# Issuing the attention sums of two score units side by side in a two-layer decoder kernel

## The chip, the cores and the metric

The kernel runs on one core of a Trainium2 chip. A core has a matrix engine (TensorE, PE in the profile; its weight loads are listed as PEld), a vector engine (VectorE, DVE), a scalar engine (ScalarE, ACT), a general engine (GpSimd, POOL) and a queue processor that issues the transfers (SyncE, SP). Each takes its own instructions in order and waits for the others by semaphores. Matrix results land in PSUM, here used as eight banks of 128 partitions by 512 float32; everything else is in on-chip buffers, which the program takes from pools.

The metric is the device time of the whole program in microseconds, as the median of several runs. One further run was recorded by the profiler; its span reaches from the first to the last instruction.

## The reference

Two decoder layers work on `x` of shape (4, 1024, 256), with a context of 77 tokens for each batch:

```python
x = x + L0_attn(layernorm(x))            # 16 heads of 16, causal softmax with ALiBi, then w_proj
x = x + L0_xattn(layernorm(x), ctx)      # 16 heads of 64 over 77 context tokens
x = x + L0_ffn(layernorm(x))             # gated, ternary weights, int8-like activations
x = x + L1_attn(layernorm(x))            # 16 heads of 16, causal, "power" attention with gates
x = x + L1_xattn(layernorm(x), ctx)      # 8 heads of 64
x = x + L1_ffn(layernorm(x))             # gated, FP4 quantised
```

The change touches the two self-attentions. In layer 0 the weights of the values are `softmax(q k / 4 + bias)`. In layer 1 they are `(|q k| + 1e-7)^2 * G_t / G_s`, where G is a running product of gates, divided by their sum. In both, the output of a query is the sum of the values times these weights, over all earlier keys.

## The kernel before

**Stages.** The program goes through the batches twice. In the first phase it does layer 0's self-attention (`A0`) of batch b, interleaved with the cross-attention and the feed-forward of batch b-1 and with the preparation of weights. In the second phase it does layer 1's self-attention (`A1`), interleaved with the rest of layer 0 for the last batch and then with layer 1's cross-attention and feed-forward. Python generators yield after each small piece of work, and `weave` takes pieces of two generators in a given ratio. `schedule` lists who is woven with whom.

**What orders the instructions.** The interleaving only fixes the order in which instructions are written down. The program is then built by a tile framework with a scheduler that reorders each engine's instructions: it keeps what depends on data, on buffers and on explicit order edges, and among the rest picks by its own model of time. So the order on the engines is not that of the source.

**Score units.** A self-attention works on groups of four heads (g = 0 to 3) and on chunks of 256 queries (c = 0 to 3). For a chunk, each block of 128 keys (j) that it may see is one unit. The unit's scores, for keys by queries, are made for two heads at a time in a PSUM bank S (lines 392 to 394 in `A0`, 867 in `A1`). In `A0`, ScalarE takes the exponential into a buffer P (line 395). In `A1`, VectorE or ScalarE takes the absolute value into P (lines 873 and 871), ScalarE squares all of P (line 875), and for the two blocks at the diagonal POOL multiplies by a decay (line 878). P holds 4 heads by 256 queries and its pool has four buffers.

**Sums.** The function `pv` adds a unit to the result: for each of the four heads a matmul whose stationary operand is 32 columns wide, that head's values with a column of ones, and whose moving operand is P. Each head writes 32 of the 128 partitions of the PSUM bank O, so four matmuls stand beside each other in the array (line 404 in `A0`, line 895 in `A1`). The trace lists each of these float32 matmuls twice. In `A1`, off-diagonal sums use values that POOL has first scaled by gate factors: a memset and a multiplication into a buffer VsJ (lines 855 and 857), of which there are three. When the last unit of a chunk pair (`A0`) or a chunk (`A1`) has been added, `o_out` or `out` takes O out of PSUM, transposes and divides it.

**The lag.** A unit whose scores have been written down is put in the queue `pend`. Once there are more than two (`LAG0`, `LAG1`), the oldest is taken out and its `pv` is written down. This happens after each unit:

```python
for c, j in units:
    pend.append((pv, (c, j) + scores(c, j)))
    if len(pend) > self.LAG0:
        f, a = pend.popleft()
        f(*a)
    yield
```

In `A1` the same loop also calls `local`, which makes the exponentials of running gates for half of the queries (lines 831 and 832, read in `out`), as soon as the oldest waiting unit belongs to the new half.

Beside this, `A0` also computes the maxima of the next head group's scores (`a0_max`: matmuls at line 346, masks at 350, VectorE's maximum at 351), which go into the next group's exponent.

Of the kernel before, what the change touches and what calls it, by code (L numbers as in the profile page):

```python
# [89 lines left out]

class Kern:
    MAGIC = 12582912.0
    LAG0, LAG1 = 2, 2
    GQ, NQ = (2, 2, 2, 2), (12, 12, 12, 12)
    NW = ((25, 25, 38, 38),) * 4

# [26 lines left out]
        self.xs = {}  # L123
        self.ready = {}

    BUFS = {"X": 4, "V": 4, "QS": 2, "KS": 2, "P": 4, "ot": 2, "q4s": 2, "qr": 2, "VsJ": 3, "wst": 2, "E": 2, "kh": 1, "qp": 2, "EX": 2}


    BANKS = (
# [16 lines left out]
    def t(self, shape, dt, tag, alt=None):  # L146
        self.n += 1
        tag = (alt or {}).get(tag, tag)
        if tag[0] == "_":
            return self.sb.tile(shape, dt, tag=tag, name=f"s{tag}_{self.n}", bufs=2)  # L150
        return self.sb.tile(shape, dt, tag=tag, name=f"{tag}_{self.n}", bufs=self.BUFS.get(tag, 1))

# [226 lines left out]
    def a0_main(self, st, V, y, g, O, pend):  # L379
        nc = self.nc  # L380
        units = [(c, j) for c in range(4) for j in range(2 * c + 2)]

        def scores(c, j):
            q0 = max(j, 2 * c) * 128
            w = (2 * c + 2) * 128 - q0
            dg = j >= 2 * c
            P = self.t([128, 4, 256], F32, "P")
            for p in range(2):
                S = self.p("S").rearrange("p (h k) -> p h k", h=2)
                for e in range(2):  # L390
                    hh = 2 * p + e
                    nc.tensor.matmul(S[:, e, 0:w], st[1][:110, hh, j * 128 : (j + 1) * 128], st[0][:110, hh, q0 : q0 + w], start=e == 0, stop=not dg and e == 1)  # L392
                if dg:
                    nc.tensor.matmul(S[:, :, 0:128], self.identb, self.maskTb.unsqueeze(1).to_broadcast([128, 2, 128]), start=False, stop=True)
                nc.scalar.activation(P[:, 2 * p : 2 * p + 2, 256 - w :], S[:, :, 0:w], AF.Exp)  # L395
            return P, 256 - w

        def pv(c, j, P, o0):
            if c % 2 == 0 and j == 0:
                O[0] = self.p("O")  # L400
            o = (c % 2) * 256
            for hh in range(4):
                h = g * 4 + hh
                nc.tensor.matmul(O[0][hh * 32 : hh * 32 + 32, o + o0 : o + 256], V[j // 4][:, j % 4, h * 17 : h * 17 + 32], P[:, hh, o0:], start=c % 2 == 0 and j == 0, stop=c % 2 == 1 and j == 2 * c + 1)  # L404
            if c % 2 == 1 and j == 2 * c + 1:
                self.o_out(O[0], y, g, c // 2)

        for c, j in units:
            pend.append((pv, (c, j) + scores(c, j)))
            if len(pend) > self.LAG0:  # L410
                f, a = pend.popleft()
                f(*a)
            yield

    def o_out(self, O, y, g, ch):
# [400 lines left out]
    def a1_main(self, b, V, dr, gt, cs):  # L816

        nc = self.nc
        ew, W, DL, DR, ub = gt
        Ds, O, st = {}, {}, {}  # L820
        chunks = [(g, c) for g in range(4) for c in cs]

        def load_gates(g, c, new):
            if new:
                for s in range(2):
                    nc.sync.dma_start(DL[s][3:15], W[g].rearrange("p (h j) n -> (p h) (j n)", h=4))
            nc.sync.dma_start(DR[0:3].rearrange("k h j t -> k h (j t)"), W[g].rearrange("p (h j) n -> p h (j n)", h=4)[:, :, c * 256 : c * 256 + 256])

        def local(g, k):
            S = self.p("D")  # L830
            nc.tensor.matmul(S, self.ind, DL[0][:, k * 512 : (k + 1) * 512], start=True, stop=True)
            nc.scalar.activation(ub, S, AF.Exp)

        def decay(g, c):
            Dt = self.t([128, 2, 4, 128], F32, "y1")
            for k in range(2):
                j = 2 * c + k
                pd = self.p("D").rearrange("p (h t) -> p h t", h=4)
                for s in range(2):
                    q = slice(s * 64, s * 64 + 64)  # L840
                    nc.tensor.matmul(pd[:, :, q], DL[s][:, j * 128 : (j + 1) * 128], DR[:, :, k, q], start=s == 0, stop=s == 1)
                nc.scalar.activation(Dt[:, k], pd, AF.Exp)
            Ds[g, c] = Dt

        def scores(g, c, j):
            hs = slice(g * 4, g * 4 + 4)
            q0 = max(j, 2 * c) * 128
            w = (2 * c + 2) * 128 - q0
            P = self.t([128, 4, 256], F32, "P")
            i0 = max(j + 1, 2 * c)  # L850
            ni = 2 * c + 2 - i0
            Vs = None
            if ni:
                Vs = self.t([128, 2, 83], F32, "VsJ")
                nc.gpsimd.memset(Vs[:, :ni, 68:83], 0.0)
                o = self.eo(j) + i0 - j - 1
                nc.gpsimd.tensor_tensor(
                    Vs[:, :ni, 0:68].rearrange("p i (h e) -> p i h e", h=4),
                    V[j // 4][:, j % 4, g * 68 : g * 68 + 68].rearrange("p (h e) -> p h e", h=4).unsqueeze(1).to_broadcast([128, ni, 4, 17]),
                    ew[:, o : o + ni, hs].unsqueeze(3).to_broadcast([128, ni, 4, 17]),  # L860
                    ALU.mult,
                )
            for p in range(2):
                S = self.p("S").rearrange("p (h k) -> p h k", h=2)
                for e in range(2):
                    hh = 2 * p + e
                    nc.tensor.matmul(S[:, e, 0:w], st[g][1][:96, hh, j * 128 : (j + 1) * 128], st[g][0][:96, hh, q0 : q0 + w], start=e == 0, stop=e == 1)  # L867
                Pv = P[:, 2 * p : 2 * p + 2, 256 - w :]
                self.absn += 1
                if self.absn % 8 in ABS_ACT:  # L870
                    nc.scalar.activation(Pv, S[:, :, 0:w], AF.Abs)
                else:
                    nc.vector.tensor_reduce(Pv, S[:, :, 0:w].unsqueeze(3), AX.X, ALU.max, apply_absolute_value=True)  # L873
            Pw = P[:, :, 256 - w :]
            nc.scalar.activation(Pw, Pw, AF.Square, bias=self.eps1)  # L875
            if j >= 2 * c:
                Pd = P[:, :, 256 - w : 384 - w]
                nc.gpsimd.tensor_tensor(Pd, Pd, Ds[g, c][:, j - 2 * c], ALU.mult)  # L878
            return P, Vs, i0

        def pv(g, c, j, P, Vs, i0):
            if j == 2 * c:
                O[g, c] = self.p("O")
            Oc = O[g, c]
            fin = (c > 0 and j == 2 * c - 1) or (c == 0 and j == 1)
            for i in range(max(j, 2 * c), 2 * c + 2):
                c0 = (i - 2 * c) * 128
                for hh in range(4):
                    h = g * 4 + hh
                    r = slice(hh * 32, hh * 32 + 32)  # L890
                    if i == j:
                        lhs, o0 = V[j // 4][:, j % 4, h * 17 : h * 17 + 32], 256 + c0
                    else:
                        lhs, o0 = Vs[:, i - i0, hh * 17 : hh * 17 + 32], c0
                    nc.tensor.matmul(Oc[r, o0 : o0 + 128], lhs, P[:, hh, c0 : c0 + 128], start=j == 2 * c and i == 2 * c, stop=fin and i == 2 * c + 1)  # L895
            if fin:
                out(g, c)
# [20 lines left out]
        pend = deque()  # L918
        need = None
# [3 lines left out]
        for n, (g, c) in enumerate(chunks):  # L923
            units = [2 * c, 2 * c + 1] + list(range(2 * c))
            nxt = chunks[n + 1] if n + 1 < len(chunks) else None
            if nxt and nxt[0] == g:
                load_gates(*nxt, False)
            if c == cs[0] and g < 3:
                st[g + 1] = self.stacks(g + 1, dr, False)
            if c % 2 == 0:  # L930
                need = (g, c // 2)
            for m, j in enumerate(units):
                pend.append((g, c, j) + scores(g, c, j))
                if len(pend) > self.LAG1:
                    pv(*pend.popleft())
                if need and (pend[0][0], pend[0][1] // 2) == need:
                    local(*need)
                    need = None
                if nxt:
                    if nxt[0] != g and m == 1:  # L940
                        load_gates(*nxt, True)
                    if m == (len(units) - 1 if nxt[0] != g else min(3, len(units) - 1)):
                        decay(*nxt)
                yield
        while pend:
            pv(*pend.popleft())
            yield

# [320 lines left out]
```

## Time and profile before

| | us |
|---|---|
| median of 3 runs | 2577.97 (2571.63 to 2580.77) |
| profiled execution | 2593.41 |
| its span | 2591.4 |
| TensorE busy | 2214.7 (85% of the span) |
| VectorE busy | 1769.4 (68%) |
| ScalarE busy | 1592.7 (61%) |
| POOL busy | 1227.5 (47%) |
| stage of `A0`'s sums, 164 to 1355 us | TensorE busy 1070.28 of 1191 |
| stage of `A1`'s sums, 1355 to 2445 us | TensorE busy 917.87 of 1090 |

Busy time counts an engine's instructions where they overlap only once. "Idle before" is the time that an engine stood still just ahead of an instruction, with what ended it; "issue" there means that the profile shows nothing that was waited for. The chain of waits is followed back from the last instruction to whatever released each one, so that its parts add up to the span. A line such as L189 can be that of a helper: L189 is the three-term matmul of split float32 operands that projections, cross-attention and feed-forward all use.

### The profile page before, as it was taken

How to read it: one execution, taken by the hardware profiler on the slowest of the kernel's cores; microseconds unless marked ns; L12 is line 12 of the kernel's file. 1: busy time of each engine (PE TensorE's matmuls, PEld its weight loads, DVE VectorE, ACT ScalarE, POOL GpSimd, SP SyncE). 2: the span in 40 equal slices, each digit the busy share in tenths (PEclk: the TensorE clock that was granted, in tenths of full speed). 3: DMA queues.
4: the chain of work that ended last, by engine and by line, in shares of the span. 5: the costliest groups of instructions: out<-in, count | busy, mean ns of one | idle time of the engine just before them, and what ended most of it. 6: DMA issues, size and time to landing. Idle time of an engine off the chain costs nothing.

```text
span 2591.4 us, 51361 instructions
## 1 busy us (share of the span) xinstructions
PE 2214.7 (85%) x19057; PEld 1575.9 (61%) x19094; DVE 1769.4 (68%) x3865; ACT 1592.7 (61%) x4099; POOL 1227.5 (47%) x2026
## 2 busy tenths in 40 slices
PE   5698889988989999899887997798879887879887
PEld 4455446754556755566545774476667666757676
DVE  3556555667566577566777677678857886677787
ACT  3255435666656676556666996786658674867532
POOL 6121302144321242213446467657875677565665
PEclk9689889999999999999997998898989998979888
DMA  8856540223652225122262211521162215333000
GB/s 228 184 133 178 163 103 13 68 62 108 158 146 58 67 81 183 41 68 55 73 189 80 73 53 64 168 83 47 64 167 72 57 65 165 86 111 83 10 9 17
DMA packets 170287, 248.44 MB, mean 96 GB/s; under 512 B 13734, under 2 KB 146166, under 8 KB 161430
## 3 DMA queue, kind: packets, MB, share of 16 engines
q1 hardware_dynamic: 170038, 245.17, 34.9%
q8 instruction: 150, 2.46, 0.4%
q14 instruction: 99, 0.81, 0.1%
HBM read 162.65 MB, written 82.21 MB: 94 GB/s over the span
## 4 chain that ended last, share of the span: by engine, by line
PE 50%; DVE 17%; DMA 13%; POOL 7%; ACT 5%; issue 3%; SPq 1%; POOLq 0%; ACTq 0%; DVEq 0%
PE T L189 8%; PE W L189 7%; PE O L404 6%; PE Q L189 4%; PE M L346 4%; PE S L392 4%; PE O L895 4%; PE S L867 3%; DMA KS<-c_alk 2%; DVE P L873 2%; DMA MD<-R 2%; DVE s_mt L351 2%; DMA UD<-R 1%; DMA QS<-dr 1%; PE T L716 1%
## 5 line engine op out<-in xcount | busy, mean ns | idle before, releaser
L351 DVE TENSOR_REDUCE s_mt<-M 128x1 f32<-128x512 f32 (+3 forms) x608 | 386.4, 656 | 161.7 <-PE M L350 112.8
L395 ACT ACTIVATE P<-S 128x512 f32<-128x512 f32 (+1 forms) x640 | 342.0, 564 | 167.5 <-PE S L392 87.1
L875 ACT ACTIVATE P<-P,eps 128x1024 f32<-128x1024 f32 (+1 forms) x320 | 341.6, 1091 | 68.5 <-DVE P L873 66.0
L873 DVE TENSOR_REDUCE P<-S 128x512 f32<-128x512 f32 (+1 forms) x480 | 281.4, 609 | 62.9 <-PE S L867 55.5
L189 PE MATMUL T<-R,xX 128*128 128x308 f32 (+1 forms) x1328 | 303.6, 340 | 13.2 <-DMA R<-g1d 3.1
L346 PE MATMUL M<-KS,QS 108*128 108x512 bf16 (+3 forms) x768 | 229.5, 347 | 54.7 <-DVE s_mt L351 21.3
L616 POOL TENSOR_TENSOR E<-E,s_xsm 128x616 f32<-128x616 f32 x88 | 108.3, 1231 | 323.5 <-DVE s_xsm L614 209.3
L392 PE MATMUL S<-QS,KS 110*128 110x256 bf16 (+1 forms) x1280 | 232.0, 270 | 27.9 <-ACT P L395 14.3
L613 ACT ACTIVATE E<-T,s_xmx 128x77 f32<-128x77 f32 x704 | 223.9, 361 | 41.4 <-DVE s_xmx L610 35.5
L189 PEld LDWEIGHTS T<-R,xX 128*128 128x128 f32 x1328 | 221.3, 197 | 42.4 <-ACT E L613 8.7
L189 PE MATMUL W<-R,xph 128*128 128x256 f32 (+2 forms) x1192 | 241.2, 299 | 4.3 <-DVE xpl L178 3.3
L867 PE MATMUL S<-QS,KS 96*128 96x256 bf16 (+1 forms) x1280 | 213.3, 273 | 35.1 <-DVE P L873 24.8
L404 PE MATMUL O<-P,V 128*32 128x256 f32 (+1 forms) x2560 | 241.4, 376 | 0.0
L189 PEld LDWEIGHTS W<-R,xph 128*128 128x128 f32 (+2 forms) x1192 | 195.0, 200 | 17.0 <-DVE xpl L178 4.9
L878 POOL TENSOR_TENSOR P<-P,y 128x512 f32<-128x512 f32 x128 | 168.2, 1320 | 68.0 <-ACT P L875 40.5
L189 PE MATMUL W<-R,xpl 128*128 128x256 f32 (+2 forms) x596 | 178.4, 299 | 3.3 <-DVE xpl L178 3.2
L392 PEld LDWEIGHTS <-KS 110*128 110x128 bf16 x1280 | 105.2, 100 | 110.2 <-issue 54.2
L867 PEld LDWEIGHTS <-KS 96*128 96x128 bf16 x1280 | 104.1, 100 | 102.3 <-issue 73.4
L613 ACT ACTIVATION_READ_ACCUMULATOR E<-T,s_xmx 128x1 f32 x704 | 166.1, 242 | 0.0
L177 ACT ACTIVATE xph<-W 104x128 fp32r<-104x128 f32 (+1 forms) x228 | 102.4, 475 | 97.1 <-PE W L627 35.3
L895 PE MATMUL O<-P,VsJ 128*32 128x128 f32 x3584 | 157.0, 282 | 5.3 <-ACT P L875 3.5
L346 PEld LDWEIGHTS <-QS 108*128 108x128 bf16 x768 | 69.4, 102 | 131.7 <-issue 103.2
(357 smaller groups left out, 5493.3 us busy)
## 6 DMA issues: line engine op xcount, KB each, us to landing
QS<-dr SPq DMA_DIRECT2D x72, 384.0 KB
KS<-dr SPq DMA_DIRECT2D x72, 384.0 KB
dr<-qp SPq DMA_DIRECT2D x32, 768.0 KB
MD<-R SPq DMA_DIRECT2D x24, 616.0 KB
UD<-R SPq DMA_DIRECT2D x24, 616.0 KB
R<-MD SPq DMA_DIRECT2D x22, 616.0 KB
R<-UD SPq DMA_DIRECT2D x22, 512.0 KB
R<-g1d SPq DMA_DIRECT2D x6, 1408.0 KB
```

The lines of the kernel that those rows point to most:

```text
L189: nc.tensor.matmul(out, x, y, start=first and n == 0, stop=last and n == len(seq) - 1)
L346: nc.tensor.matmul(Sv[:, x, 0:w], QS[:108, hh, i * 128 : (i + 1) * 128], KS[:108, hh, k0:k1], start=x == 0, stop=not diag and x == n - 1)
L351: nc.vector.tensor_reduce(out, Sv[:, :, 0:w], AX.X, ALU.max)
L392: nc.tensor.matmul(S[:, e, 0:w], st[1][:110, hh, j * 128 : (j + 1) * 128], st[0][:110, hh, q0 : q0 + w], start=e == 0, stop=not dg and e == 1)
L395: nc.scalar.activation(P[:, 2 * p : 2 * p + 2, 256 - w :], S[:, :, 0:w], AF.Exp)
L404: nc.tensor.matmul(O[0][hh * 32 : hh * 32 + 32, o + o0 : o + 256], V[j // 4][:, j % 4, h * 17 : h * 17 + 32], P[:, hh, o0:], start=c % 2 = ...
L613: nc.scalar.activation(E[:, n * 77 : (n + 1) * 77], Sv[:, k, :], AF.Exp, bias=mx[:, n : n + 1], accum_out=sm[:, n : n + 1])
L867: nc.tensor.matmul(S[:, e, 0:w], st[g][1][:96, hh, j * 128 : (j + 1) * 128], st[g][0][:96, hh, q0 : q0 + w], start=e == 0, stop=e == 1)
L873: nc.vector.tensor_reduce(Pv, S[:, :, 0:w].unsqueeze(3), AX.X, ALU.max, apply_absolute_value=True)
L875: nc.scalar.activation(Pw, Pw, AF.Square, bias=self.eps1)
L878: nc.gpsimd.tensor_tensor(Pd, Pd, Ds[g, c][:, j - 2 * c], ALU.mult)
L895: nc.tensor.matmul(Oc[r, o0 : o0 + 128], lhs, P[:, hh, c0 : c0 + 128], start=j == 2 * c and i == 2 * c, stop=fin and i == 2 * c + 1)
```

## The change

There are three edits.

- After a unit's scores, nothing is taken from `pend` until four units wait in it (`LAG + PAIR`). Then the two oldest are summed, one after the other. So pairs are written down at every second unit.
- The two sums are traced inside `issue_after`, with the newest unit's last score matmul (`self.lead`). It adds order edges for the scheduler: what the block puts on TensorE must stand behind that matmul in TensorE's order. The edge concerns issue order alone; there is no semaphore, and other engines are not touched. In `A1`, `local` is now called inside the block, just ahead of the first sum that belongs to the new half, and also when the queue is emptied at the end.
- The pool VsJ has five buffers instead of three, since up to four units wait with their scaled values.

```diff
-    LAG0, LAG1 = 2, 2
+    LAG0, LAG1, PAIR = 2, 2, 2
...
-    BUFS = {"X": 4, ..., "P": 4, ..., "VsJ": 3, ...}
+    BUFS = {"X": 4, ..., "P": 4, ..., "VsJ": 5, ...}
...
-                    nc.tensor.matmul(S[:, e, 0:w], st[1][:110, hh, ...
+                    self.lead = nc.tensor.matmul(S[:, e, 0:w], st[1][:110, hh, ...
                 if dg:
-                    nc.tensor.matmul(S[:, :, 0:128], self.identb, ...
+                    self.lead = nc.tensor.matmul(S[:, :, 0:128], self.identb, ...
...
-            if len(pend) > self.LAG0:
-                f, a = pend.popleft()
-                f(*a)
+            if len(pend) >= self.LAG0 + self.PAIR:
+                with self.tc.issue_after(self.lead.ins):
+                    for _ in range(self.PAIR):
+                        f, a = pend.popleft()
+                        f(*a)
...
-                    nc.tensor.matmul(S[:, e, 0:w], st[g][1][:96, hh, ...
+                    self.lead = nc.tensor.matmul(S[:, e, 0:w], st[g][1][:96, hh, ...
...
-                if len(pend) > self.LAG1:
-                    pv(*pend.popleft())
-                if need and (pend[0][0], pend[0][1] // 2) == need:
-                    local(*need)
-                    need = None
+                if len(pend) >= self.LAG1 + self.PAIR:
+                    with self.tc.issue_after(self.lead.ins):
+                        for _ in range(self.PAIR):
+                            if need and (pend[0][0], pend[0][1] // 2) == need:
+                                local(*need)
+                                need = None
+                            pv(*pend.popleft())
...
         while pend:
+            if need and (pend[0][0], pend[0][1] // 2) == need:
+                local(*need)
+                need = None
             pv(*pend.popleft())
```

More of the change, by code (lines that the diff above doesn't have):

```diff
@@ L124, in __init__ @@
         self.ready = {}
-    BUFS = {"X": 4, "V": 4, "QS": 2, "KS": 2, "P": 4, "ot": 2, "q4s": 2, "qr": 2, "VsJ": 3, "wst": 2, "E": 2, "kh": 1, "qp": 2, "EX": 2}
+    BUFS = {"X": 4, "V": 4, "QS": 2, "KS": 2, "P": 4, "ot": 2, "q4s": 2, "qr": 2, "VsJ": 5, "wst": 2, "E": 2, "kh": 1, "qp": 2, "EX": 2}
     BANKS = (
@@ L391, in scores @@
                     hh = 2 * p + e
-                    nc.tensor.matmul(S[:, e, 0:w], st[1][:110, hh, j * 128 : (j + 1) * 128], st[0][:110, hh, q0 : q0 + w], start=e == 0, stop=not dg and e == 1)
+                    self.lead = nc.tensor.matmul(S[:, e, 0:w], st[1][:110, hh, j * 128 : (j + 1) * 128], st[0][:110, hh, q0 : q0 + w], start=e == 0, stop=not dg and e == 1)
                 if dg:
-                    nc.tensor.matmul(S[:, :, 0:128], self.identb, self.maskTb.unsqueeze(1).to_broadcast([128, 2, 128]), start=False, stop=True)
+                    self.lead = nc.tensor.matmul(S[:, :, 0:128], self.identb, self.maskTb.unsqueeze(1).to_broadcast([128, 2, 128]), start=False, stop=True)
                 nc.scalar.activation(P[:, 2 * p : 2 * p + 2, 256 - w :], S[:, :, 0:w], AF.Exp)
@@ L866, in scores @@
                     hh = 2 * p + e
-                    nc.tensor.matmul(S[:, e, 0:w], st[g][1][:96, hh, j * 128 : (j + 1) * 128], st[g][0][:96, hh, q0 : q0 + w], start=e == 0, stop=e == 1)
+                    self.lead = nc.tensor.matmul(S[:, e, 0:w], st[g][1][:96, hh, j * 128 : (j + 1) * 128], st[g][0][:96, hh, q0 : q0 + w], start=e == 0, stop=e == 1)
                 Pv = P[:, 2 * p : 2 * p + 2, 256 - w :]
```

## The prediction

> **What bounds the kernel now.** I read the page first, then the chain of waits by stage, then the busy time by stage, and last the time line of TensorE around the instructions that the change moves. From the page:
>
> ```profile
> span 2591.4 us, 51361 instructions
> PE 2214.7 (85%) x19057; PEld 1575.9 (61%) x19094; DVE 1769.4 (68%) x3865; ACT 1592.7 (61%) x4099; POOL 1227.5 (47%) x2026
> L404 PE MATMUL O<-P,V 128*32 128x256 f32 (+1 forms) x2560 | 241.4, 376 | 0.0
> L895 PE MATMUL O<-P,VsJ 128*32 128x128 f32 x3584 | 157.0, 282 | 5.3 <-ACT P L875 3.5
> ```
>
> TensorE (PE) is the busiest engine. The sums that the change moves are L404 (layer 0, called A0 here) and L895 (layer 1, A1; 1024 more of its matmuls stand under O<-P,V with 59.1 us). The two stages, cut where L404 ends at 1355 us (busy time by stretch, and the chain of waits for each of the same stretches, shares of the stretch):
>
> ```profile
> core 0: us, PE busy (x) PEld busy (x) DVE busy (x) ACT busy (x) POOL busy (x), PEclk, DMA share, GB/s
> 164.00:1355.00 1191.00, 1070.28 (x8347) 687.86 (x8370) 773.97 (x1681) 711.20 (x2017) 346.72 (x493) 0.94 0.38 101
> 1355.00:2445.00 1090.00, 917.87 (x9473) 704.64 (x9480) 796.95 (x1787) 780.30 (x1818) 726.54 (x1327) 0.91 0.31 87
> ```
>
> ```profile
> by line: PE O L404 12.1%; PE S L392 8.1%; PE M L346 8.0%; PE Q L189 7.1%; PE T L189 6.6%; PE W L189 6.4%; DMA KS<-c_alk 5.3%; DMA MD<-R 4.5%; DVE s_mt L351 3.6%; DMA UD<-R 2.8%; issue 2.4%; PE T L716 2.3%; PE M L350 1.9%; PE S L394 1.7%; PE
> ```
>
> The reader is to see two things. In A0 TensorE is busy 1070 of 1191 us while VectorE and ScalarE have a third free; and the first entry of the chain there is L404 itself, 12.1% of 1191 = 144 us. In A1 (84% busy) the same chain gives L895 8.7% of 1090 = 95 us, with VectorE, POOL and transfers taking larger parts.
>
> Why L404 is dear is in the time line of TensorE (start, length, instruction, count). The first seven lines are from A0, the last four from A1:
>
> ```profile
> 999.85 0.38 PE L392 MATMUL S<-QS,KS 110*128 110x256 bf16 x2
> 1000.16 0.41 PE L404 MATMUL O<-P,V 128*32 128x128 f32 x2
> 1000.50 0.38 PE L189 MATMUL Q<-WAh,yTh 128*128 128x256 f32 x1
> ...
> 1010.11 0.28 PE L392 MATMUL S<-QS,KS 110*128 110x128 bf16 x2
> 1010.23 0.27 PE L394 MATMUL S<-maskTb,identb 128*128 128x256 bf16 x1
> 1010.43 0.64 PE L404 MATMUL O<-P,V 128*32 128x256 f32 x8
> 1011.00 0.39 PE L392 MATMUL S<-QS,KS 110*128 110x256 bf16 x2
> ...
> 2006.53 0.27 PE L909 MATMUL U<-ident,ot 128*128 128x128 f32 x1
> 2006.73 0.43 PE L895 MATMUL O<-P,V 128*32 128x128 f32 x8
> 2006.97 0.40 PE L895 MATMUL O<-P,VsJ 128*32 128x128 f32 x8
> 2007.31 0.39 PE L867 MATMUL S<-QS,KS 96*128 96x256 bf16 x2
> ```
>
> These are narrow matmuls (128*32: 32 columns of the array, four beside each other). Each stands twice in the trace, since 1280 in the program give 2560 rows. Ordinary matmuls follow each other every 0.11 us here, but between the last ordinary one and the first narrow one pass 0.20 us (1010.23 to 1010.43), and on the way back at least 0.20 us more. One whole unit, 8 rows of 256 columns, takes 1010.23 to 1011.00 = 0.77 us.
>
> **The change, part by part.** *What is added and removed.* No arithmetic: the built programs have the same 15,499 matmuls, and equal counts on every other engine and on SP. Only order and two buffers differ, so the price is one of order.
>
> *Fixed cost of a run.* Call narrow matmuls that follow each other a run. Over the runs of the trace, the median from the last ordinary start to the next ordinary start is 0.559 us for 8 rows of 128 columns (37 runs), 0.786 for 16 (115, as at 2006.53 to 2007.31), and 0.997 for 24 (28). Each further set of 8 rows so costs 0.215 us, which leaves 0.344 us fixed; 8 rows of 256 columns (0.774, 194 runs) agree: 0.344 + 0.430. An ordinary matmul would take 0.11 us of the 0.344, so one run less saves 0.235 us.
>
> *Number of runs.* I compared the order of TensorE's instructions in both built programs. A0: 401 runs before, 191 after. Before, 124 runs have only 2 of a unit's 4 matmuls and 24 have only one; 238 have 4. After, 135 runs have 8, two whole units. A1: 262 before, 235 after, because most runs there were whole units already and are mixed.
> - Fixed: 210 x 0.235 = 49.4 us in A0, 27 x 0.235 = 6.3 us in A1.
> - Streaming: two of four tiles take as long as four (2 matmuls of 256 columns: 0.754 us, 16 runs). With the widest tile of each run at 0.215 us per 128 columns, A0's runs stream 154.6 us before and 132.9 after, A1's 129.9 and 128.4: 21.7 + 1.5 us.
> - Sum of TensorE time: 71.1 us in A0, 7.8 us in A1.
>
> [...] (waits: who, for what, us in all, times, longest):
>
> ```profile
> PEld O L404 <- issue: 78.3, 382, 0.4
> PEld O L895 <- issue: 33.0, 153, 0.7
> ```
>
> 382 times the narrow weight load of L404 waited 0.2 us for nothing else that the profile shows. I take the row's 0.235 us. [...]
>
> *What of it lies on the path.* L404 is 144 us of the chain and 232.4 us of busy time in its stage, 62%. L895 is 95 of 192.6 us, half. So 71.1 x 0.62 + 7.8 x 0.5 = 44 + 4 = 48 us. The rest lies beside what the chain shows as transfers (KS<-c_alk alone 5.3% of A0) or VectorE, and none of those gets shorter.
>
> *The added wait.* Sums now stand behind the newest unit's last score matmul. In the built order of A0 a unit's sums stood behind the scores of one later unit (299 of 320), afterwards behind two or three (156 each). Queued behind the waiting matmul on TensorE is everything else: side work and the next scores. That matmul waits for its score bank, which the exponential at L395 empties; TensorE waited 14.3 us for that in all. I cost this at nothing because the wait existed before; what is new is that no sums can fill it, at most those 14.3 us again.
>
> *The P buffers.* P has four buffers. Three were held at most (two pending and the newest), now four, so the exponential of the next unit needs the P that the oldest pending sum frees. In A0 the wait of ACT for L404 at L395 does not appear among the waits at all; in A1 it is 16.1 us already (ACT P L871 12.7, DVE P L873 3.4, both for L895). Lower bound 0, upper bound treated as the slower rival; I take 0 in A0, since sums stand on TensorE ahead of the scores that need the buffer, and a few us in A1.
>
> *Five VsJ buffers.* POOL's memset L855 waits 160.9 us (102 times) for L895 with three buffers. A longer lag with three could not work; with five the wait should shrink. On the chain the two lines of VsJ have 9.6 us. Bounds: 0 to 10 us gained; I take 3, which cancels the few us of P.
>
> *local(), moved ahead of the first sum of its pair.* Up to 16 times (first chunk of each head group and batch) its exponential, 0.63 us at L832, and its matmul, 0.3 us, can stand right before a use: 0 to 15 us, taken as 0, since VectorE has other work. The O bank changes no owner within a pair: 6, 14 and the A1 chunks' 2c+2 units are all even.
>
> Sum: 2591.4 - 48 = 2543 us of span, 2545 with the 2 us around it (profiled run 2593.4). The median shown is 2578.0, 0.6% below that run; so 2578 - 48 = 2530.
>
> **The rivals.**
> 1. *All of it arrives* (78.9 us, and VsJ's 10): 2490. For: A0's TensorE is 90% busy. Against: 225 us of A0's chain are transfers.
> 2. *Others take the bound*: with TensorE faster, the maxima at L351 (386 us of VectorE, 161.7 us idle before) and the exponentials hold the pace, or the whole new order, which the scheduler drew up afresh on all engines, eats it. About 10 us remain: 2568.
> 3. *Slower: P runs out.* P is written, squared (L875, 1.09 us), for diagonals multiplied on POOL (L878, 1.32 us), and only then summed. With no buffer in reserve, A1's writers L873 and L871 wait for the sums, and the sums for the newest scores. It cancels the gain from 48/320 = 0.15 us per A1 unit on; today it is 16.1/320 = 0.05. At five times today's, 80 us, minus 48 plus the 16 there: 2594; I put 2600. Against: the average unit in A1 was already summed 2 to 3 units later, and the built order moves that little (47 to 58 matmuls in between).
> 4. *The change does little*, because the scheduler had paired already: true of A1, excluded for A0 by the run counts.
>
> **How the numbers follow.** Half of it arrives: 0.50, 2530, own range 2508 to 2556. All: 0.17, around 2490. Absorbed: 0.14, 2556 to 2586. Slower: 0.19, around 2600 with a tail to 2650. A measurement here tells 0.3% (8 us) from no change. Faster: 0.50 + 0.17 + half of 0.14 = 0.74; same: 0.07; slower: 0.19. The range 2485 to 2605 leaves out some 0.07 below and 0.09 above.
>
> **What would show it.** Right: L404's busy time near 241 - 35 us, PEld O L404 <- issue at about half of its 382 times, A0's stretch shorter by some 45 us and A1's by under 10; POOL's wait at L855 well under 160.9. Wrong: A0 as long as before with PE idle more (rival 2); ACT P L395 or DVE P L873 waiting for PE O (rival 3); or the transfers KS<-c_alk and MD<-R growing on the chain.

## The result, and the profile after

The changed kernel takes 2591.4 us (median of 8 runs, 2588.4 to 2605.9) against 2577.7 us (8 runs, 2571.6 to 2584.0): the ratio is 1.0062, interval 1.0044 to 1.0081. It is slower by 0.6%, where 2530 us had been forecast.

The page after the change:

```profile
span 2588.7 us, 51317 instructions
PE 2148.5 (83%) x19094; PEld 1596.3 (62%) x19094; DVE 1752.9 (68%) x3865; ACT 1595.8 (62%) x4099; POOL 1223.3 (47%) x2026
L404 PE MATMUL O<-P,V 128*32 128x256 f32 (+1 forms) x2560 | 178.3, 374 | 2.7 <-ACT P L395 2.7
L897 PE MATMUL O<-P,VsJ 128*32 128x128 f32 x3584 | 154.0, 284 | 4.6 <-ACT P L877 4.6
```

TensorE is busy 66 us less than in the trace shown before (2214.7), and 51 us less than in a second trace of the kernel before (2199.1, below). L404 is 63 us less than in either. From the waits, the narrow loads of layer 0 and POOL's wait for the sums (lines behind layer 0's loop stand two further down in this kernel: L895 and L855 are L897 and L857):

```profile
PEld O L404 <- issue: 41.4, 198, 0.5
POOL VsJ L857 <- PE O L897: 159.4, 113, 6.1
```

382 waits of the narrow load have become 198. The time line of TensorE shows a pair: sixteen rows of 256 columns in one run, with 1.20 us from the last full matmul's start (1010.21) to the next one's (1011.41):

```profile
1010.21 0.27 PE L394 MATMUL S<-maskTb,identb 128*128 128x256 bf16 x1
1010.41 1.07 PE L404 MATMUL O<-P,V 128*32 128x256 f32 x16
1011.41 0.39 PE L346 MATMUL M<-KS,QS 108*128 108x512 bf16 x1
```

Two runs of one unit took 2 x 0.77 us. So the saving on TensorE is real, and yet the program is longer. The first profiled execution of the kernel before was itself 21 us longer than the second, so the stages are compared with the second. Busy time by stage, of the kernel before (second execution), cut where layer 0's last sum leaves PSUM, where layer 1's last does, and at the end:

```profile
153.00:1336.00 1183.00, 1066.30 (x8402) 682.56 (x8427) 779.45 (x1693) 715.56 (x2027) 348.27 (x495) 0.95 0.37 103
1336.00:2425.00 1089.00, 916.34 (x9461) 706.28 (x9472) 795.69 (x1785) 779.55 (x1817) 725.01 (x1326) 0.91 0.31 87
2425.00:2571.00 146.00, 109.98 (x675) 102.08 (x674) 117.80 (x229) 44.67 (x146) 91.64 (x104) 0.87 0.03 12
```

and after the change:

```profile
151.00:1329.00 1178.00, 1022.31 (x8426) 711.13 (x8425) 773.87 (x1696) 712.01 (x2025) 348.58 (x496) 0.93 0.38 103
1329.00:2433.00 1104.00, 916.05 (x9466) 708.40 (x9466) 788.56 (x1786) 785.01 (x1816) 724.72 (x1325) 0.91 0.31 86
2433.00:2589.00 156.00, 112.58 (x676) 105.99 (x676) 114.44 (x223) 45.49 (x146) 88.00 (x104) 0.82 0.03 11
```

The columns are the stretch, its length, then busy time of PE, PEld, DVE, ACT and POOL, the granted clock, the share of the DMA engines and GB/s. There are two questions. In layer 0's stage TensorE is busy 44 us less, but the stage is only 5 us shorter. In layer 1's stage it is busy as long as before, and the stage is 15 us longer; the end takes 10 more, so that 25 us are lost behind layer 0.

### The profile page after: what moved, and what is told of

It is laid out like the page before. It is cut to its first block, busy times and chain, and to the rows that moved or that the text cites. A ratio compares the mean times of both kernels' runs of the same rounds, so it can differ in the third digit from the quotient of the medians.

```text
span 2588.7 us, 51317 instructions
## 1 busy us (share of the span) xinstructions
PE 2148.5 (83%) x19094; PEld 1596.3 (62%) x19094; DVE 1752.9 (68%) x3865; ACT 1595.8 (62%) x4099; POOL 1223.3 (47%) x2026
## 4 chain that ended last, share of the span: by engine, by line
PE 46%; DVE 19%; DMA 18%; POOL 7%; ACT 6%; issue 3%; SPq 1%; POOLq 0%; ACTq 0%; DVEq 0%
PE T L189 8%; PE W L189 8%; PE O L404 5%; PE Q L189 4%; PE S L392 3%; PE O L897 3%; DMA MD<-R 3%; PE M L346 3%; PE S L869 3%; DMA UD<-R 3%; DMA KS<-c_alk 2%; DVE P L875 2%; DVE s_mt L351 2%; DMA y<-locd 2%; DMA QS<-VsJ 1%
## 5 line engine op out<-in xcount | busy, mean ns | idle before, releaser
L395 ACT ACTIVATE P<-S 128x512 f32<-128x512 f32 (+1 forms) x640 | 338.6, 567 | 118.3 <-PE S L394 64.8
L392 PE MATMUL S<-QS,KS 110*128 110x256 bf16 (+1 forms) x1280 | 232.4, 269 | 45.4 <-DMA QS<-VsJ 23.6
L189 PE MATMUL W<-R,xph 128*128 128x256 f32 (+2 forms) x1192 | 249.1, 306 | 10.0 <-DVE xpl L178 8.3
L189 PEld LDWEIGHTS W<-R,xph 128*128 128x128 f32 (+2 forms) x1192 | 202.5, 207 | 18.7 <-DVE xpl L178 9.7
L392 PEld LDWEIGHTS <-KS 110*128 110x128 bf16 x1280 | 111.4, 101 | 119.2 <-issue 48.5
L189 PE MATMUL W<-R,xpl 128*128 128x256 f32 (+2 forms) x596 | 183.6, 308 | 1.4 <-DVE xpl L178 1.4
L404 PE MATMUL O<-P,V 128*32 128x256 f32 (+1 forms) x2560 | 178.3, 374 | 2.7 <-ACT P L395 2.7
L615 ACT ACTIVATION_READ_ACCUMULATOR E<-T,s_xmx 128x1 f32 x704 | 160.8, 230 | 0.0
L177 ACT ACTIVATE xph<-W 128x512 fp32r<-128x512 f32 (+1 forms) x228 | 99.9, 469 | 97.9 <-PE W L629 34.8
L897 PE MATMUL O<-P,VsJ 128*32 128x128 f32 x3584 | 154.0, 284 | 4.6 <-ACT P L877 4.6
```

What stands on the lines that cost most here:

```text
L189: nc.tensor.matmul(out, x, y, start=first and n == 0, stop=last and n == len(seq) - 1)
L392: self.lead = nc.tensor.matmul(S[:, e, 0:w], st[1][:110, hh, j * 128 : (j + 1) * 128], st[0][:110, hh, q0 : q0 + w], start=e == 0, stop=no ...
L615: nc.scalar.activation(E[:, n * 77 : (n + 1) * 77], Sv[:, k, :], AF.Exp, bias=mx[:, n : n + 1], accum_out=sm[:, n : n + 1])
```

## The experiments

Each ratio below is to runs of the kernel before that were measured together with that experiment; their medians lie between 2573.6 and 2584.0 us. So ratios can be compared between experiments, and microseconds only within one.

### A second trace of the kernel before

> The kernel before, profiled a second time. Its first profiled execution took 2593.4 us, 15 us over its median of 2578, while the changed kernel's profiled execution (2590.6) is at its median of 2591. If the first trace was a slow one, this one has a span near 2576 and its stages (layer 0's attention ends at 1356 us in the first trace) end earlier; then part of the 26 us by which layer 0's attention seemed shorter after the change is not the change's. If it is again near 2590, the stage times of the first trace stand.

It took 2572.5 us with a span of 2570.3. Layer 0's last sum left PSUM at 1336.2 us instead of 1356.2. So of the 27 us that the first trace shows between the two kernels at that point, 20 belong to that one execution.

### Which part of the change is slower

The two loops are independent in the built order: with one of them changed, the other layer's runs on TensorE are those of the kernel before or nearly so. Layer 0 alone (this edit and the next are against the changed kernel):

```diff
             if len(pend) >= self.LAG0 + self.PAIR:      # layer 0: as changed
...
-                if len(pend) >= self.LAG1 + self.PAIR:
...
+                if len(pend) > self.LAG1:               # layer 1: as before
+                    pv(*pend.popleft())
...
-    BUFS = {..., "VsJ": 5, ...}
+    BUFS = {..., "VsJ": 3, ...}
```

> Pairs and order edges in layer 0's attention only; layer 1's loop and the three VsJ buffers as before. Built order: A0 191 narrow runs, A1 264. Theory 1 (A0 gains, A1's pairing and what follows it give the gain back): about 26 us faster than before, ratio near 0.990. Theory 2 (A0's gain is spent wherever it is made, since the second phase is held by other engines and by the order drawn up afresh): within 8 us of before, ratio 0.997 to 1.003. Theory 3 (A0's pairing is itself the loss, and the first trace only hid it): slower, ratio 1.005 or more.

Measured: 2566.9 us, ratio 0.9983 (0.9965 to 1.0000). It is not slower, and it gains 4 us by the ratio (8 by the medians) rather than 26. The number is theory 2's; its reason, that the second phase spends the gain, is not borne out: the gain is already missing at the end of layer 0's own stage (below).

Layer 1 alone, with five VsJ buffers:

```diff
-            if len(pend) >= self.LAG0 + self.PAIR:
...
+            if len(pend) > self.LAG0:                   # layer 0: as before
+                f, a = pend.popleft()
+                f(*a)
```

> Pairs and order edges in layer 1's attention and five VsJ buffers; layer 0's loop as before. Built order: A0 401 narrow runs as before, A1 237. Theory 1: slower by 15 to 40 us, ratio 1.006 to 1.015, because the held-back sums keep P buffers, and VectorE's and ScalarE's waits at the lines that write P grow. Theory 2: within 8 us of before. Theory 3: equal or slightly faster, ratio 0.995 to 1.000.

Measured: 2611.8 us, ratio 1.0152 (1.0130 to 1.0175), 37 to 39 us slower. The loss is made in layer 1. That P buffers are its cause, as the expectation said, is not borne out below. The two halves do not add up: minus 4 and plus 39 us would make 35, and the whole change loses 16. Why the loss is smaller in company is open.

The buffers alone:

```diff
-    BUFS = {..., "VsJ": 3, ...}
+    BUFS = {..., "VsJ": 5, ...}
```

> The kernel before with five VsJ buffers and nothing else. Built order: A0 401 narrow runs, A1 278. Theory 1: within 5 us of before; POOL's wait at its memset for the sums, 160.9 us with three buffers, stays above 100 us, as it did in the changed kernel with five (159.4), so that the loss is the pairing's. Rival: the two more buffers alone change layer 1's order for the worse, 10 us or more slower.

Measured: 2570.3 us, ratio 0.9985 (0.9970 to 0.9999), and POOL's wait at the memset was 175.0 us in layer 1's stage, more than with three (158.8 in the second trace). The buffers are not the loss. Nor do they shorten the wait they seemed made for: over the whole program it is 159 to 184 us in the kernels with three buffers and 149 to 182 in those with five. What sets it is open.

### What in layer 1 is slower

The changed kernel without its order edges:

```diff
-                with self.tc.issue_after(self.lead.ins):
+                if True:
...
-                    with self.tc.issue_after(self.lead.ins):
+                    if True:
```

> The changed kernel without its order edges: pairs are written down, five VsJ buffers, but the scheduler may put a sum wherever it likes. Built order: A0 401 narrow runs as before, A1 271. Theory P (in layer 1 the edge holds sums behind scores, so that buffers and outputs come late, and this costs the 37 us): the loss goes with the edge, within 8 us of before. Rival L (the loss is in local() now standing right ahead of its first use, or in the source order of pairs): still slower by 20 us or more, since local() and the pairs are written down as in the changed kernel.

Measured: 2576.0 us, ratio 1.0008 (0.9992 to 1.0024). The loss is gone. So is the effect in layer 0: the built order has 401 runs there again, as many as before. Writing two sums down together does nothing by itself; only the edge makes a pair.

Then the place of `local`. Layer 1's pairs with their edges and layer 0 as before, but `local` outside the edge and before the pair is due:

```diff
                     with self.tc.issue_after(self.lead.ins):
                         for _ in range(self.PAIR):
-                            if need and (pend[0][0], pend[0][1] // 2) == need:
-                                local(*need)
-                                need = None
                             pv(*pend.popleft())
+                if need and (pend[0][0], pend[0][1] // 2) == need:
+                    local(*need)
+                    need = None
...                                                     # nor when the queue is emptied
```

> Layer 1's pairs with their edges and five VsJ buffers, layer 0 as before, but local() is called outside the edge, after a pair has been taken out, when the oldest waiting unit belongs to the new half, as in the kernel before. With the late local() this took 2611.8 us, ratio 1.0152. Rival L: most of the 37 us comes back, ratio under 1.005, ScalarE's wait for local's matmul (ACT y L832 <- PE D L831, 17.7 us) is gone. Theory P: the loss stays, ratio 1.010 or more.

Measured: 2578.6 us, ratio 1.0022 (1.0011 to 1.0034). Of the 1.52%, 1.30% (33 us) came back from moving one matmul and one exponential, which the program does 32 times. The stage of layer 1 is 1122 us with the late `local` and 1083 with the early one, at nearly the same TensorE work (923 and 919 us). The waits of ScalarE and VectorE that bear on it, first with the late `local`, then with the early one, and last ScalarE's wait for `local` in the changed kernel (L834 there):

```profile
ACT y L832 <- PE D L831: 17.7, 13, 6.1
ACT P L871 <- PE O L895: 17.1, 14, 3.8
DVE P L873 <- PE O L895: 10.6, 15, 2.7
```

```profile
ACT P L871 <- PE O L895: 43.4, 17, 8.5
DVE P L873 <- PE O L895: 4.7, 8, 1.8
ACT y L832 <- PE D L831: 2.0, 4, 0.7
```

```profile
ACT y L834 <- PE D L833: 12.9, 9, 4.3
```

Line 832 is `local`'s exponential and 831 its matmul. Behind the edge the matmul stands on TensorE after the newest unit's scores; the exponential, already at the head of ScalarE's queue, waits for it up to 6.1 us (up to 4.3 in the changed kernel), and ScalarE starts nothing of what stands behind it: the traces of the kernel before and of the changed one have ScalarE's work in the order of the built program (2047 and 2042 entries, alike neighbours counted once, none out of place). The kernel before had 2.0 us of this wait in all. Worked out from the traces, the result of `local` lay ready a median of 9.6 us before its first reader in the kernel before, 10.7 us with the early `local`, and 4.9 us with the late one. The lines at 871 and 873 are the waits for a free P: they are longer where the kernel is faster (48.1 us against 27.7). P was not what cost.

Two things limit this account. The 17.7 us are about half of the 33, and 12.9 of the changed kernel's 19; the rest was not found in any one wait. And a late result alone does not cost: in the changed kernel without edges it lay ready a median of 7.5 us before its reader (4.5 with the edges), for the first chunk of a head group only 1.2 us (1.0), and that kernel is at 1.0008.

Is it the edge, or that `local` is written down later? The same kernel with `local` at the late place, but outside the edge:

```diff
                 if len(pend) >= self.LAG1 + self.PAIR:
+                    if need and (pend[0][0], pend[0][1] // 2) == need:
+                        local(*need)
+                        need = None
                     with self.tc.issue_after(self.lead.ins):
                         for _ in range(self.PAIR):
-                            if need and (pend[0][0], pend[0][1] // 2) == need:
-                                local(*need)
-                                need = None
                             pv(*pend.popleft())
```

> Layer 1's pairs with their edges and five VsJ buffers, layer 0 as before. local() is written down at the late place, just ahead of its pair, but outside the edge, so that the scheduler may issue its matmul earlier than the newest scores. If the edge on local()'s matmul is the loss: near the early local(), ratio under 1.006. If the late place in the source is enough: near 1.015, as with the edge.

Measured: 1.0046 (1.0034 to 1.0057), so 1.06% of the 1.30% is the edge on `local`'s matmul; the 0.24% left for the later place is little more than the intervals can tell from nothing.

And the other way round, the kernel before with `local` alone made late and held, no pairs and three buffers:

```diff
                 if len(pend) > self.LAG1:
+                    if need and (pend[0][0], pend[0][1] // 2) == need:
+                        with self.tc.issue_after(self.lead.ins):
+                            local(*need)
+                        need = None
                     pv(*pend.popleft())
-                if need and (pend[0][0], pend[0][1] // 2) == need:
-                    local(*need)
-                    need = None
...                                                     # and when the queue is emptied
```

> The kernel before with nothing but local() moved: traced just ahead of the first sum of the new half and held by the edge behind the newest unit's scores. No pairs, three VsJ buffers. If the late local() costs its 33 us by itself, ratio 1.008 or more and ScalarE waits at L832 for local's matmul well over 2.0 us. If it takes the pairs to make it late enough to hurt, within 8 us of before.

Measured: 1.0065 (1.0039 to 1.0091), 17 us, which lies between the two forecasts. It costs by itself, though half of what it costs among layer 1's pairs. ScalarE's own wait at L832 was only 4.2 us here, against the forecast of "well over 2.0", so most of the 17 us is not that wait. In seven of the 32 cases the reader takes the result within 0.04 us of its end; the trace shows 1.6 us of waiting for it there. What the rest consists of is open.

Last, the whole change with `local` put back (the edit of the early `local`, in the changed kernel):

> The changed kernel with one thing put back: local() is called outside the edge, after a pair has been taken out, as before. The changed kernel is 1.0062 of before. If the place of local() inside the edge is the whole of the loss, layer 0's pairs (0.9983) and layer 1's pairs with the early local() (1.0022) add up to about 1.000: 2568 to 2582 us, at least 10 us faster than the changed kernel. If it was the two kinds of pairs together, it stays above 1.004.

Measured: 0.9990 (0.9974 to 1.0006). The place of `local`, in the edge or out of it, is the whole of the loss: 0.72%, 19 us. What is left is a change that saves TensorE 42 us in its trace (2157.4 against 2199.1) and the program nothing that can be measured.

### Where layer 0's saving went

TensorE in layer 0's stage, before and with layer 0's pairs alone. Before, in the second trace, it was busy 1066.30 of 1183 us (the row 153.00:1336.00 above). What it waited for there:

```profile
PE M L346 <- DVE s_mt L351: 19.7, 32, 3.5
PE M L346 <- DMA KS<-c_alk: 19.1, 6, 5.6
PE S L392 <- ACT P L395: 12.3, 17, 3.6
PE S L392 <- DMA QS<-VsJ: 11.9, 4, 4.1
```

With layer 0's pairs, busy time by stretch and waits:

```profile
152.00:1328.00 1176.00, 1017.15 (x8399) 709.01 (x8422) 773.17 (x1695) 710.78 (x2024) 348.01 (x494) 0.93 0.38 103
```

```profile
PE M L346 <- DMA KS<-c_alk: 33.9, 7, 6.2
PE S L392 <- DMA QS<-VsJ: 22.5, 5, 5.8
PE M L346 <- DVE s_mt L351: 22.0, 44, 3.2
PE S L392 <- ACT P L395: 21.8, 24, 3.9
```

Busy time fell by 49 us and the stage by 7; the other 42 are idle. One pair of traces is thin evidence for 7 us, since two traces of the kernel before differ by more than that. Worked out from all kept traces with the loads in place, from the first to the last time that layer 0's sums leave PSUM: the eight without pairs in layer 0 take 1183 to 1199 us, the four with pairs 1177 to 1182. On average the stage is 11 us shorter, TensorE is busy 50 us less and idle 39 us more.

The transfers KS<-c_alk, the last of a head group's load of queries and keys, and QS<-VsJ, the two rows of maxima, hold TensorE 25 us longer, in about as many waits as before (12 against 10), and the exponentials 10 us longer. One such load, before and then with layer 0's pairs, in the time lines of the transfer queue and of TensorE:

```profile
1099.97 0.78 SPq L317 DMA_DIRECT2D QS<-dr  x2
1112.06 0.38 PE L346 MATMUL M<-KS,QS 108*128 108x128 bf16 x4 [1.77 <-DMA KS<-c_alk]
```

```profile
1095.97 0.77 SPq L317 DMA_DIRECT2D QS<-dr  x2
1108.11 0.58 PE L346 MATMUL M<-KS,QS 108*128 108x128 bf16 x4 [4.71 <-DMA KS<-c_alk]
```

The load is issued as TensorE's matmuls on the buffers' former content end (in the first trace of the kernel before ten such loads, and in the changed kernel's eight, start within 0.1 us of the end of the L394 that they wait for), and its first reader starts 12.1 us later in both. What differs is how much of the 12.1 us TensorE fills with other work. Over all waits for KS<-c_alk in the stage the median from issue to reader is 12.1 us before (6 cases) and 12.2 with pairs (7). If the narrow runs had only been covering loads of a fixed duration, the saving must appear once there are none. Two kernels leave the loads out for 14 of layer 0's 16 head groups, which then compute with other heads' values:

```diff
     def stacks(self, g, dr, alibi):
+        if alibi:
+            self.held = getattr(self, "held", [])
+            self.turn_s = getattr(self, "turn_s", -1) + 1
+            if len(self.held) == 2:
+                return self.held[self.turn_s % 2]
...
             nc.sync.dma_start(KS[96:110], self.c["alk"][:, g * 4 : g * 4 + 4, :])
+            self.held.append((QS, KS))
```

> The kernel before, leaving out the loads of the stacked queries and keys for 14 of layer 0's 16 head groups (the first two groups' are used again), so that these groups compute with other heads' values. No transfer is left to wait for at the start of a group except the two rows of maxima. Together with the next kernel it asks where layer 0's gain went. Expected 25 to 60 us faster than before (KS<-c_alk has 62 us of the chain in layer 0's stage); this alone tells no theory from another.

> Layer 0's pairs alone, with the same loads left out as in the kernel above. With the loads, pairing took 49 us of TensorE's busy time out of layer 0's stage and shortened it by 7. Theory C (the narrow runs had covered the loads; what TensorE no longer does it now waits for them): without the loads the gap between unpaired and paired grows from 8 us to 25 us or more. Rival (VectorE's maxima, ScalarE's exponentials and the lower granted clock hold the stage, whatever the loads): the gap stays under 15 us.

Measured: 2527.2 us (0.9815, 0.9777 to 0.9854) without pairs and 2466.8 us (0.9586, 0.9552 to 0.9620) with them. The gap between unpaired and paired, 4 us by the ratios with the loads (8 by the medians), is 60 us without them. Layer 0's stage, without pairs and then with them:

```profile
151.00:1277.00 1126.00, 1051.04 (x8423) 674.94 (x8421) 766.01 (x1687) 711.10 (x2026) 345.77 (x493) 0.97 0.28 85
```

```profile
153.00:1232.00 1079.00, 989.46 (x8419) 693.73 (x8418) 763.34 (x1686) 707.53 (x2023) 349.36 (x496) 0.97 0.29 89
```

TensorE's busy time falls by 62 us and the stage by 47, three quarters of it; the other 8 us by which the spans differ lie outside the stage. VectorE and ScalarE do almost the same work (763 and 708 us) in a stage that is 97 us shorter, so they were not the limit. Most of layer 0's gain goes into the wait for the loads. The granted clock is higher in both kernels without loads (0.97), so the test takes the waits and the clock that goes with them together.

How much arrives depends on the rest of the program: the pairs of layer 0 are worth 4 us beside the old loop of layer 1, 8 beside layer 1's pairs with the early `local` (1.0022 to 0.9990), 13 beside five VsJ buffers alone (0.9985 to 0.9934) and 23 beside layer 1's pairs with the late one (1.0152 to 1.0062).

### A version that beats both

Layer 0's pairs and five VsJ buffers, with layer 1's loop as before:

```diff
-    BUFS = {..., "VsJ": 3, ...}
+    BUFS = {..., "VsJ": 5, ...}       # in the kernel with layer 0's pairs alone
```

> Pairs and edges in layer 0's attention, five VsJ buffers, layer 1's loop as before: the two parts of the change that were not slower alone (0.9983 and 0.9985). If they add up, ratio 0.997, near 2562 us, which beats both kernels; if not, 0.998 to 1.002.

Measured: 2564.3 us, ratio 0.9934 (0.9911 to 0.9957). It is faster than both kernels, and by more than the two parts together (0.9968), though by little more than the intervals. In its trace layer 0's sums end at 1334 us, no earlier than in the other kernels with pairs. Each build is ordered afresh by the scheduler, and where these two gain together is open.

## Why the prediction was wrong

**The saving on TensorE: right in kind, too large in size.** 71.1 us had been worked out for layer 0. L404's busy time fell by 59.4 us in the stage (234.7 to 175.3) and the number of waits of its load halved, as the order of the built program had said. All other matmuls together took 10 us more (831.6 to 841.9), at a clock of 0.93 instead of 0.95, so that 49 us were left. The streaming had been worked out at 21.7 us for layer 0, so that by this estimate most of the 59.4 us was the fixed cost of the runs. In layer 1, where 7.8 us had been worked out, nothing measurable went (916.3 and 916.1 us). One reading is off without consequence: the row of 0.754 us with 16 runs is that of a single matmul of 256 columns; two take 0.760 (83 runs), and four 0.774, so fewer tiles still save next to nothing.

**"What of it lies on the path": the step that failed for layer 0.** The prediction took L404's share of the chain, 62%, as the share of a saving that reaches the end, and said of the transfers that "none of those gets shorter". It is true that none gets shorter. But a transfer that starts when TensorE reaches a certain point and is used as long after it as before (12.1 us, and 12.2 with pairs) makes the wait longer by what TensorE no longer does meanwhile. With loads 7 of 49 us arrived in the stage (11 of 50 over all traces), without them 47 of 62. A share of the chain says where time lay, not what a saving there is worth. The sign that had been named for this, KS<-c_alk growing on the chain, could not appear: the chain holds the transfer, which stayed at 62 us (5.2% of 1183, then 5.3% of 1176), and what grew was TensorE's wait for it. Another transfer, UD<-R, went from 22 to 45 us of the chain in these two traces (33 in the first trace); its loads were still made when the gain arrived without those of the head groups. Rival 2 (something else takes the bound) had the size nearly right, 10 us, but named VectorE and ScalarE; it was the loads.

**The added wait for the score bank** had been taken as 0, with 14.3 us as the most. TensorE's waits for L395 at L392 rose from 12.3 to 21.8 us, inside that bound.

**"`local()`, moved ahead of the first sum of its pair": the step that failed for layer 1, and it decides the sign.** The bounds were 0 to 15 us, "taken as 0, since VectorE has other work". By itself the move costs 17 us, in the changed kernel 19, and among layer 1's pairs alone 33. The estimate looked at the reader on VectorE, and that reader waited only 2.4 us for it in the changed kernel. It left out that the edge holds whatever the block puts on TensorE, `local`'s matmul too (1.06 of the 1.30%), and that ScalarE, whose work ran in the built order, stands still at the exponential behind it: 12.9 us in the changed kernel, against 2.0 before. How the remainder of the 19 us comes about is open.

**The P buffers (rival 3).** The waits for L895 rose from 11.7 us in the second trace to 26.3 after the change, and to 48.1 with the early `local`. That kernel is 5.7 us slower than before, and no run shows how much of it is P's. So the waits are there, below the 80 us that the rival asked, and the program was slower for another reason. That the rival's 2600 us lie near the measured 2591.4 is luck.

**Five VsJ buffers.** 3 us had been taken and 4 were measured, at the edge of the noise and by luck: POOL's wait, the reason given, did not shrink.

**Rival 4** (the scheduler had paired already) was rightly excluded for layer 0: the run without edges shows that only the edge made pairs there.

## What to carry to other kernels

Before an engine's saving is counted, ask of each transfer in the stage whether it starts at a point that the engine reaches and lasts as long as before: the saving can then turn into a wait (here 42 of 49 us became idle time), and the test is to take the transfers away, with which 47 of 62 us arrived. An order edge around a block binds everything that the block puts on that engine, also the small producer that other engines need early (among layer 1's pairs the edge on `local`'s matmul cost 1.06%); keep such work out of the block. Change one thing at a time in a program that is reordered as a whole: here a gain of 4 to 23 us and a loss of some 19 came in one diff.

## What was not expected of the hardware

Where ordinary matmuls follow each other at 0.11 us, 0.20 us pass from the last ordinary start to the first narrow one, and 0.205 us (128 columns) or 0.31 us (256 columns) from the last narrow start to the next ordinary one. These are the medians over the runs of the trace, before and with pairs alike, so going from one kind to the other takes TensorE 0.09 us more on the way in than staying with ordinary ones. Halving the runs of L404, and filling them, took 59 us from its busy time.

The granted clock of TensorE fell where its waits grew, from 0.95 to 0.93 in layer 0's stage with pairs, and was 0.97 in both kernels without loads. Gaps of more than 3 us before a matmul sum to 39 us in the stage before and 68 us with pairs. The load shown above is a single case: after the wait of 1.77 us the clock was 1.00 from 1105.3 to 1118.9 us, and around the wait of 4.71 us it was 0.50 from 1105.5 to 1112.1. By the trace's clock records, all 15 gaps of more than 3 us with pairs lie at a stretch of half clock (granted clock 0.5), or within 1 us of one. In the first trace of the kernel before and in the changed kernel's, ordinary bf16 matmuls of 256 columns follow each other at 0.11 us where the granted clock is 1.0 and at 0.21 us where it is 0.5. An estimate of the price comes from that and from the time that TensorE worked at half clock, 89 us before and 108 with pairs: if half of it is lost, 10 us more are lost with pairs, which fits the 10 us that other matmuls took longer. What starts a half-clock stretch is not shown: in layer 0's stage, 12 of the 22 in the first trace of the kernel before and 9 of the 23 in the changed kernel's begin with no gap of more than 3 us in the 8 us before them.
